# A Mamba and feed-forward kernel: two compares move to VectorE, the first block is reordered, the last block gets a path of its own

## The chip, the cores and the metric

The kernel runs on one core of a Trainium2 chip. The metric is the device time of one execution in microseconds (us). A core has five engines with a queue each, and each queue is worked off in order: TensorE (PE; its weight loads are listed as PEld), VectorE (DVE), ScalarE (ACT), GpSimd (POOL) and SyncE (SP), which here issues almost all DMAs. An instruction that waits holds up everything behind it in its queue.

## The reference

The input x has 2 sequences of 4096 tokens with 256 numbers each, all fp32. Two layers follow one another, both with a layer norm ahead and behind, and a residual:

```python
x = x + layernorm(mamba(layernorm(x)))
x = x + layernorm(ffn(layernorm(x)))

# mamba, 512 channels, 16 states
xp, z = split(x @ W_in.T);  xp = silu(xp)
B, C, dt_in, lam_in = split(xp @ W_x.T)         # 16, 16, 1, 1 columns
B, C = rmsnorm(B + B_bias), rmsnorm(C + C_bias)
dt = softplus(dt_in * W_dt + b_dt);  lam = sigmoid(lam_in)
B, C = rotate(B, C by the running sum of mean(dt))
dA = exp(-exp(A_log) * dt)
h[t] = dA[t] * h[t-1] + u[t]      # u from lam, dt, dA, B, xp of t and t-1
y = sum over states of h * C;  y = (y + xp * D) * silu(z)
return y @ W_out.T

# ffn, hidden 1024; ternary(w): the sign of w where |w| is over half its mean, times the mean
h = gelu(ln(x) @ ternary(w1).T + b1)
return ln(h) @ ternary(w2).T + b2
```

## The kernel before

The 8192 tokens are worked off in 16 blocks of 512. In a block the recurrence is 64 **units**: 4 groups of 128 channels (j), 4 rounds of states (q), 4 parts (c). Every unit is one scan on VectorE (`unit_scan`, L997 and L1000) over 512 tokens in 128 lanes. Its decay dA comes from ScalarE into one of four PSUM banks (`decay`, pool `ps_da`), its input from GpSimd as a product of b and v (`inputs`, L984, two units at a time). Afterwards the states are multiplied by c, partly on VectorE (L1014), partly on GpSimd (L1010), and TensorE sums them over the states into the bank of y (`sum_states`, L1026). There are three buffers of scan inputs; the sum frees one. After the 16 units of a channel group `gate` (L1036) multiplies y by silu(z).

The order of the work is written out by hand. Each unit has three **places**; the tables `AT`, `AT_FIRST`, `LAG` and `W_AT` give every step its place, and the program issues the steps in that order, so that each engine's queue follows it. While block k is scanned, `plan_ahead` prepares block k+1 (layer norm, projection, b, c, dt, v) and `plan_behind` finishes block k-1 (output projection, norm, the feed-forward layer). `AT_FIRST` is the table for block 0; its negative places lie before the first scan. After the last block 100 more units of places are run through with no scans, so that `plan_behind` finishes it.

What the steps of the change touch:

- Weights of the feed-forward layer (`ternary`, during block 0, for w1 and then w2): `above` and `below` (L410, L413) compare 128x2048 weights with plus and minus half of their mean on GpSimd, `signs` (L418) subtracts the two on GpSimd in two halves, `factors` (L423) scales two columns there; then TensorE sums the offsets (`offsets`, L445 and L466), VectorE adds them to the bias (L455, L476), ScalarE applies the gains (L456, L479).
- First block: `project` (L612) and `keep` (L626) make eight projections; the first four are copied to `xp`, on which `silu_x` then runs as one activation of 128x2048 (L225). `bc_project` (L643) multiplies `xp` by W_x, 128 tokens after another, each over all four channel groups. From its columns come dt (`dt_project`, `dt_row`, `dt_spread`, `softplus`), its transposes with sums (`dt_turn` L733, `dt_keep` L741), b and c (`bc_take` to `bc_store`), and v (`weigh` L865, `weigh_x` L880). dt, v, b and c are stored to DRAM (L708, L881, L812) and loaded back into lanes (`load_ch` L950 for dt and v, `load_bc` L939 for b and c), four DMAs per load. Several functions are loaded into ScalarE as tables (ACT_TABLE_LOAD); `special` (L225, with L221 for exp and ln) is the helper for these.
- Last block: `out_project` (L1044), `out_square` (L1056), `out_power`, `residual` (L1067), the norm (`Norm`: L557, L558, L562, L567, L572), its transposes (L586, L593), `ffn_1` and `ffn_keep` (L1072, L1083), `gelu` (L225), `ffn_2` (L1094, L1103, L1111), `ffn_sums` (L1120, L1124), `ffn_out` (L1132), `ffn_square` (L1141), `ffn_scale` (L1152), `finish` (L1156) and the store of half a block (L1157). The result of `ffn_2` for 128 tokens lies in the only bank of the pool `ps_ff`; the projections use the two banks of `ps_mm`.

Of the kernel before, what the change touches and what calls it, by code (L numbers as in the profile page):

```python
# [125 lines left out]
    "a_stats": (-60, -60),  # L126
    "a_power": (-60,),
    "a_offset": (-60,),
    "a_apply": (-60, -60),
    "a_turn": (-60, -60),  # L130
    "a_evict": (-60, -60),
    "project": (-59, -58, -57, -56, 16, 2, 2, 0),
    "keep": (-58, -57, -56, -55, 18, 3, 5, 0),
    "silu_x": (-54,),
    "bc_project": (-53, -53),
    "bc_take": (-52,),
    "dt_project": (-51,),
    "bc_square": (-50,),
    "bc_power": (-48,),
    "dt_row": (-49,),  # L140
    "dt_spread": (-48,),
    "softplus": (-47,),
    "bc_scale": (-46,),
    "dt_sum": (-45,),
    "dt_turn": (-46, -46, -46, -46),
    "dt_keep": (-46, -46, -46, -46),
    "angles": (-44,),
    "diag_lam": (-43,),
    "diag_rem": (-42,),
    "silu_z": (57,),  # L150
    "sines": (-40,),
    "rotate_a": (-37,),
    "rotate_b": (-36,),
    "bc_turn": (-34,),
    "bc_store": (-33,),
    "dot_sum": (-26,),
    "dot_shift": (0,),
    "dot_take": (0,),
    "weigh": (-41, 4, 10, 15),
    "weigh_x": (-35, 5, 11, 18),  # L160
# [3 lines left out]
    "load_dt": (-34,),  # L164
    "load_v": (-32,),
    "load_b": (-31, -20, 15, 3),
    "load_c": (-30, -20, 9, 4),
# [4 lines left out]
def mamba_ffn_kernel(  # L172
# [207 lines left out]
    def ternary(src, wide, nk, width, cols):  # L380
# [28 lines left out]
        def above():  # L409
            nc.gpsimd.tensor_scalar(q, w, t["scale"], 0.5, ALU.mult, ALU.is_gt)  # L410

        def below():
            nc.gpsimd.tensor_scalar(w, w, t["scale"], -0.5, ALU.mult, ALU.is_lt)  # L413
# [180 lines left out]

    class Block:
# [24 lines left out]
    def keep(s, e):  # L620
        if e == 0:
            s.xp = p1.tile([P, NJ, T], F32, tag="xp", name=f"xp_{s.k}")
            s.zs = {}
        if e >= NJ:
            s.zs[e - NJ] = p1.tile([P, T], F32, tag="zs", name=f"zs_{s.k}_{e - NJ}", bufs=8)
        nc.scalar.copy(s.xp[:, e, :] if e < NJ else s.zs[e - NJ], s.pz.pop(e))  # L626

    def silu_x(s):
        special(s.xp, s.xp, AF.Silu)
        s.xlast = small.tile([P, NJ], F32, tag="xlast", name=f"xlast_{s.k}")  # L630
        nc.scalar.copy(s.xlast, s.xp[:, :, T - 1])
# [5 lines left out]
    def bc_project(s, cs):  # L637

        if cs[0] == 0:
            s.pbc = ps_ff.tile([P, NC4, 2 * NS + 2], F32, tag="ff", name=f"pbc_{s.k}")  # L640
        for c in cs:
            for j in range(NJ):
                nc.tensor.matmul(  # L643
                    s.pbc[:, c, :],
                    lhsT=s.xp[:, j, c * P : (c + 1) * P],
                    rhs=wx[:, j, :],
                    start=(j == 0),
                    stop=(j == NJ - 1),
                )

# [384 lines left out]
    def gate(s, j):  # L1035
        nc.vector.tensor_mul(s.zs[j], s.ys.pop(j), s.zs[j])  # L1036

# [25 lines left out]
    def residual(s, h):  # L1063
        po, rs = s.p2.pop(h), s.ff["rso", h]
        for i in range(2):
            xc = s.x[:, 2 * h + i, :]
            nc.vector.scalar_tensor_tensor(xc, po[:, i, :], rs[:, i : i + 1], xc, ALU.mult, ALU.add)  # L1067
# [21 lines left out]
    def ffn_2(s, c):  # L1089

        po = ps_ff.tile([P, DM + 1 + P], F32, tag="ff", name=f"pf_{s.k}_{c}")
# [66 lines left out]

    NU = NJ * NQ * NG
# [17 lines left out]
    def plan_ahead(s, prev):  # L1177
# [24 lines left out]
        add("bc_project", bc_project, s, (0, 1), i=0)  # L1202
        add("bc_project", bc_project, s, (2, 3), i=1)
# [43 lines left out]
    def plan_behind(s):  # L1247
# [4 lines left out]
        def begin():  # L1252
            s.x = x_load(s.k, "xpost")

# [94 lines left out]
    first.run(-60)  # L1349
# [17 lines left out]
    decay_rates()  # L1367
# [7 lines left out]
    for base in range(NB * NU + BEHIND):  # L1375
# [3 lines left out]
        if m == 0:  # L1379
# [4 lines left out]
            if 0 < k <= NB:  # L1384
# [16 lines left out]
        at_place(3 * base + 2)  # L1401
        if m == X_AT and k + 2 < NB:
            xnext = x_load(k + 2, "h1")

# [47 lines left out]
```

## Time and profile before

| | |
|---|---|
| median of 3 runs | 2060.76 us (2060.21 to 2062.78) |
| the profiled execution's own time | 2060.96 us |
| its span, first to last instruction | 2059.2 us |
| first scan of block 0 | 64.26 us |
| first scan of block 1, of block 2 | 228.91, 345.65 us |
| POOL's wide compares, together | 28.7 us in four instructions |
| last gate (L1036) begins | 1987.59 us |
| last `finish` (L1156) ends | 2056.10 us |

The profile comes from one execution. Its page gives the busy time of each engine, the span in 40 slices (each digit is a busy share in tenths, `PEclk` the granted clock of TensorE in tenths), the chain of work that ended last, and the costliest groups of instructions. Other views are the timeline (start, duration, engine, line, operation, output and inputs; in brackets the idle time of the engine before it and who ended it), the waits (who waited for whom), and sums over chosen windows. Durations of neighbours in a queue overlap by up to 0.1 us, so steps from start to start are what adds up.

### The profile page before, as it was taken

Reading aid. Unit: us, or ns where it says so; the run is one execution under the profiler, and the core shown is the slowest. Engines: PE = TensorE matmul, PEld = TensorE weight load, DVE = VectorE, ACT = ScalarE, POOL = GpSimd, SP = SyncE. Lnnn points to the kernel's source line nnn. Section 1 sums busy time; section 2 is a strip of 40 time slices with the busy share of each in tenths; the row PEclk is TensorE's granted clock in tenths of the full one; section 3 lists DMA queues with packets and bytes.
Section 4 is the critical chain, followed back from the end, with each engine's and each line's share of the span. In section 5 each row is a group of like instructions: output and inputs, shape, how many; then the busy total and the mean of one; then the engine's idle time right before and its main releaser. Section 6 shows DMA issues by size and latency. Waiting matters only on the chain.

```text
span 2059.2 us, 28149 instructions
## 1 busy us (share of the span) xinstructions
PE 1742.7 (85%) x8638; PEld 1036.3 (50%) x8638; DVE 1761.0 (86%) x2766; ACT 1627.1 (79%) x3344; POOL 1815.7 (88%) x1178
## 2 busy tenths in 40 slices
PE   5755788898998989898888989899898889887776
PEld 3423436464563646455453646455464646545255
DVE  1654999999898999999999999999898999989950
ACT  5664797888979798887979788887978888896743
POOL 3599999899999999899999999999999999999950
PEclk7765899999999999999999999999999999999889
DMA  3632446345463645445444644446354545545200
GB/s 79 173 92 72 114 103 165 101 100 130 114 153 88 161 102 123 108 115 149 112 126 102 165 103 111 116 119 159 96 142 103 131 108 116 140 113 151 46 21 11
DMA packets 155689, 233.39 MB, mean 113 GB/s; under 512 B 30129, under 2 KB 55793, under 8 KB 155537
## 3 DMA queue, kind: packets, MB, share of 16 engines
q1 hardware_dynamic: 153408, 230.80, 45.0%
q0 software_dynamic: 544, 0.71, 0.2%
q8 instruction: 68, 1.11, 0.2%
q14 instruction: 85, 0.69, 0.1%
q10 hardware_dynamic: 1584, 0.07, 0.1%
HBM read 188.51 MB, written 42.99 MB: 112 GB/s over the span
## 4 chain that ended last, share of the span: by engine, by line
ACT 38%; DVE 17%; POOL 12%; DMA 11%; PE 11%; issue 8%; SPq 3%; DVEq 0%; ACTq 0%; POOLq 0%
ACT da L225 12%; POOL g L984 6%; DVE g L1000 6%; DMA vr<-v_d 6%; ACT L225 5%; DVE da L997 4%; ACT L221 3%; DMA xpre<-in_L_attn_x_dram 3%; ACT h L1083 3%; POOL g L1010 2%; ACT dt L225 2%; PE pdtT L733 2%; PE y L1026 2%; ACT h L225 2%; DVE g L1014 2%
## 5 line engine op out<-in xcount | busy, mean ns | idle before, releaser
L984 POOL TENSOR_TENSOR g<-b,vr 128x1024 f32<-128x1024 f32 x512 | 1017.4, 1999 | 36.1 <-DMA c<-bc_d 12.9
L1000 DVE TENSOR_TENSOR_SCAN g<-da,ini,g 128x512 f32<-128x512 f32 x560 | 709.9, 1272 | 46.4 <-ACT da L225 30.6
L225 ACT ACTIVATE da<-dtr,aneg 128x512 f32<-128x512 f32 x1024 | 683.7, 683 | 82.6 <-DVE g L1000 44.6
L1010 POOL TENSOR_TENSOR g<-c,g 128x1024 f32<-128x1024 f32 (+1 forms) x256 | 626.8, 2451 | 64.0 <-ACT hl L1004 55.0
L997 DVE TENSOR_TENSOR_SCAN da<-da,ini,g 128x512 f32<-128x512 f32 x336 | 422.0, 1274 | 33.2 <-POOL g L984 17.8
L1026 PE MATMUL y<-g,fold 128*32 128x512 f32 x2048 | 338.7, 662 | 42.3 <-POOL g L1010 32.2
L1094 PE MATMUL pf<-w2q,h 128*128 128x257 f32 x1024 | 313.4, 388 | 25.1 <-DVE o L1132 22.0
L1072 PE MATMUL ph<-oT_h,w1q 128*128 128x512 f32 x512 | 255.7, 635 | 24.8 <-ACT oT_h L593 13.3
L612 PE MATMUL pz<-oT_a,wi 128*128 128x512 f32 x512 | 251.0, 627 | 10.4 <-ACT zs L626 4.9
L1014 DVE TENSOR_TENSOR g<-da,c 128x512 f32<-128x512 f32 x384 | 257.3, 670 | 0.0
L1103 PEld LDWEIGHTS pf<-h 128*128 128x128 f32 x1024 | 194.6, 190 | 27.2
L1103 PE MATMUL pf<-h 128*128 128x128 f32 x1024 | 196.7, 274 | 0.0
L1094 PEld LDWEIGHTS pf<-w2q,h 128*128 128x128 f32 x1024 | 155.1, 191 | 61.1 <-DVE o L1132 42.1
L1072 PEld LDWEIGHTS ph<-oT_h,w1q 128*128 128x128 f32 x512 | 94.8, 200 | 164.5 <-issue 82.3
L612 PEld LDWEIGHTS pz<-oT_a,wi 128*128 128x128 f32 x512 | 92.9, 195 | 158.6 <-issue 87.3
L1026 PEld LDWEIGHTS y<-g,fold 128*32 128x32 f32 x2048 | 49.1, 112 | 155.8 <-POOL g L1010 66.0
L1044 PE MATMUL po<-wo,zs 128*128 128x256 f32 x512 | 120.9, 390 | 0.0
L1044 PEld LDWEIGHTS po<-wo,zs 128*128 128x128 f32 x512 | 96.2, 193 | 39.9 <-issue 27.6
L1000 DVE TENSOR_TENSOR_SCAN g<-da,g 128x512 f32<-128x512 f32 x80 | 96.5, 1211 | 19.7 <-ACT da L225 11.7
L865 PE MATMUL ps<-mix,dtT 128*128 128x129 f32 (+1 forms) x512 | 81.3, 306 | 34.2 <-DVE remdot L833 27.0
L865 PE MATMUL pw<-ddot,dtT 128*128 128x128 f32 (+1 forms) x512 | 83.8, 313 | 27.8 <-DVE dx L928 22.2
L225 ACT ACT_TABLE_LOAD x80 | 102.6, 1283 | 1.4
(209 smaller groups left out, 2390.4 us busy)
## 6 DMA issues: line engine op xcount, KB each, us to landing
dtr<-dt_d SPq DMA_DIRECT2D x256, 256.0 KB, 5.0
vr<-v_d SPq DMA_DIRECT2D x256, 256.0 KB, 7.1
dt_d<-dt SPq DMA_DIRECT2D x64, 256.0 KB, 2.1
v_d<-v SPq DMA_DIRECT2D x64, 256.0 KB, 4.8
b<-bc_d SPq DMA_DIRECT2D x256, 64.0 KB, 2.1
c<-bc_d SPq DMA_DIRECT2D x256, 64.0 KB, 2.7
xpre<-in_L_attn_x_dram SPq DMA_DIRECT2D x16, 512.0 KB, 4.3
xpost<-in_L_attn_x_dram SPq DMA_DIRECT2D x16, 512.0 KB, 3.8
```

Source lines behind the costliest of these rows:

```text
L225: nc.scalar.activation(dst, src, f, **kw)
L612: nc.tensor.matmul(s.pz[e], lhsT=wi[:, kk, e * P : (e + 1) * P], rhs=s.na.oT[:, kk, :], start=(kk == 0), stop=(kk == 1),)
L984: nc.gpsimd.tensor_mul(s.g[j, q][:, hs, :], s.bcq[0, q][:, None, :].to_broadcast([P, 2, T]), s.ch[j, "vr"][:, hs, :],)
L997: nc.vector.tensor_tensor_scan(da, da, g, ini, ALU.mult, ALU.add)
L1000: nc.vector.tensor_tensor_scan(g, da, g, ini, ALU.mult, ALU.add)
L1010: nc.gpsimd.tensor_mul(g, s.bcq[1, q][:, None, :].to_broadcast([P, NG - n, T]), g)
L1014: nc.vector.tensor_mul(s.g[j, q][:, c, :], da, s.bcq[1, q])
L1026: nc.tensor.matmul(s.ys[j][c * G : (c + 1) * G, :], lhsT=fold, rhs=g[:, c, :], start=False, stop=(q == NQ - 1), skip_group_check=True,)
L1044: nc.tensor.matmul(s.p2[h][:, i, :], lhsT=s.zs[j][:, c * P : (c + 1) * P], rhs=wo[:, j, :], start=(j == 0), stop=(j == NJ - 1),)
L1072: nc.tensor.matmul(s.ph[f], lhsT=w1q[:, kk, f * P : (f + 1) * P], rhs=s.nh.oT[:, kk, :], start=(kk == 0), stop=(kk == 1),)
L1094: nc.tensor.matmul(po[:, 0 : DM + 1], lhsT=gT, rhs=w2q[:, f, :], start=(f == 0), stop=(f == NH - 1), skip_group_check=True,)
L1103: nc.tensor.matmul(po[:, DM + 1 :], lhsT=gT, rhs=gT, start=False, stop=False, skip_group_check=True,)
```

## The change

The two compares of each weight run on VectorE instead of GpSimd. In block 0 `keep` applies silu while it takes the projection from PSUM, `bc_project_first` runs group by group between the projections, the norm of b and c follows softplus, dt's load stands directly behind its stores, and b is loaded ahead of v. The last block has no `plan_behind`: `tail` does its work, by halves of 256 tokens up to the gelu, with `ph` and `pf` in the four banks of `ps_da`, and stores 128 tokens at a time; three quarters of its output projection are issued at the gate of the third channel group. `residual` also writes row sums, in every block.

```diff
 AT_FIRST = {
...
-    "project": (-59, -58, -57, -56, 16, 2, 2, 0),
-    "keep": (-58, -57, -56, -55, 18, 3, 5, 0),
-    "silu_x": (-54,),
-    "bc_project": (-53, -53),
-    "bc_take": (-52,),
-    "dt_project": (-51,),
-    "bc_square": (-50,),
-    "bc_power": (-48,),
-    "dt_row": (-49,),
-    "dt_spread": (-48,),
-    "softplus": (-47,),
-    "bc_scale": (-46,),
-    "dt_turn": (-46, -46, -46, -46),
-    "dt_keep": (-46, -46, -46, -46),
+    "project": (-78, -77, -75, -72, 16, 2, 2, 0),
+    "keep": (-76, -74, -71, -69, 18, 3, 5, 0),
+    "silu_x": (-58,),
+    "bc_take": (-67,),
+    "dt_project": (-66,),
+    "bc_square": (-61,),
+    "bc_power": (-60,),
+    "dt_row": (-65,),
+    "dt_spread": (-64,),
+    "softplus": (-63,),
+    "bc_scale": (-59,),
+    "dt_turn": (-55, -55, -55, -55),
+    "dt_keep": (-55, -55, -55, -55),
...
-    "load_dt": (-34,),
-    "load_v": (-32,),
-    "load_b": (-31, -20, 15, 3),
-    "load_c": (-30, -20, 9, 4),
+    "load_dt": (-62,),
+    "load_v": (-42,),
+    "load_b": (-43, -20, 15, 3),
+    "load_c": (-41, -20, 9, 4),
+    "bc_project_first": (-73, -70, -69, -68),
+    "decay_rates": (-57,),
 }
...
         def above():
-            nc.gpsimd.tensor_scalar(q, w, t["scale"], 0.5, ALU.mult, ALU.is_gt)
+            nc.vector.tensor_scalar(q, w, t["scale"], 0.5, ALU.mult, ALU.is_gt)
         def below():
-            nc.gpsimd.tensor_scalar(w, w, t["scale"], -0.5, ALU.mult, ALU.is_lt)
+            nc.vector.tensor_scalar(w, w, t["scale"], -0.5, ALU.mult, ALU.is_lt)
...
+        if s.k == 0 and e < NJ:
+            special(s.xp[:, e, :], s.pz.pop(e), AF.Silu)
+            return
...
+    def bc_project_first(s, j):
+        if j == 0:
+            s.pbc = ps_ff.tile([P, NC4, 2 * NS + 2], F32, tag="ff", name=f"pbc_{s.k}")
+        for c in range(NC4):
+            nc.tensor.matmul(
+                s.pbc[:, c, :],
+                lhsT=s.xp[:, j, c * P : (c + 1) * P],
+                rhs=wx[:, j, :],
+                start=(j == 0 and c == 0),
+                stop=(j == NJ - 1),
+                skip_group_check=True,
+            )
...
     def gate(s, j):
         nc.vector.tensor_mul(s.zs[j], s.ys.pop(j), s.zs[j])
+        if s.k == NB - 1 and j >= NJ - 2:
+            tail_out(s, range(NJ - 1) if j == NJ - 2 else (j,))
...
     def residual(s, h):
...
-            nc.vector.scalar_tensor_tensor(xc, po[:, i, :], rs[:, i : i + 1], xc, ALU.mult, ALU.add)
+            nc.vector.scalar_tensor_tensor(
+                xc, po[:, i, :], rs[:, i : i + 1], xc, ALU.mult, ALU.add, accum_out=s.sums[:, c : c + 1]
+            )
...
+    def tail_out(s, js):
+        for h in range(2):
+            if 0 in js:
+                s.p2[h] = mm_tile([P, 2, DM], f"po_{s.k}_{h}")
+            for j in js:
+                for i in range(2):
+                    c = 2 * h + i
+                    nc.tensor.matmul(
+                        s.p2[h][:, i, :],
+                        lhsT=s.zs[j][:, c * P : (c + 1) * P],
+                        rhs=wo[:, j, :],
+                        start=(j == 0 and i == 0),
+                        stop=(j == NJ - 1),
+                        skip_group_check=True,
+                    )
+    def tail(s):
...
+        for h in range(2):
+            out_square(s, h)
+            out_power(s, h)
+        for h in range(2):
+            cl = slice(2 * h, 2 * h + 2)
+            residual(s, h)
+            n.stats((2 * h, 2 * h + 1))
+            power(n.rs[:, cl], n.var[:, cl], n.scale, n.eps)
+            nc.vector.tensor_mul(n.nm[:, cl], n.nm[:, cl], n.rs[:, cl])
+            n.apply((2 * h, 2 * h + 1))
...
+        for h in range(2):
+            for f2 in range(NH // 2):
+                ph = ps_da.tile([P, 2, T // 2], F32, tag="da", name=f"ph_{k}_{h}_{f2}")
...
+                for i in range(2):
+                    f = 2 * f2 + i
+                    special(s.h1[:, f, half[h]], ph[:, i, :], AF.Gelu, bias=b1c[:, f : f + 1])
+        for c in range(NC4):
+            ffn_2(s, c, ps_da.tile([P, DM + 1 + P], F32, tag="da", name=f"pf_{k}_{c}"))
...
+        for c in range(NC4):
+            ffn_sums(s, c)
+            ffn_out(s, c)
+            junk = p1.tile([P, DM], F32, tag="junk", name=f"junk_{k}_{c}")
+            nc.scalar.activation(junk, s.o2[:, c, :], AF.Square, accum_out=so[:, c : c + 1])
+            power(rg[:, c : c + 1], so[:, c : c + 1], 1.0 / DM, LN_EPS)
+            xc = s.x[:, c, :]
+            nc.vector.scalar_tensor_tensor(
+                xc, s.o2[:, c, :], rg[:, c : c + 1], xc, ALU.mult, ALU.add
+            )
+            nc.sync.dma_start(tokens(out, k)[:, c, :], xc)
...
-            if 0 < k <= NB:
+            if 0 < k < NB:
                 plans.append(plan_behind(prev))
...
+        if base == NB * NU - 10:
+            tail_load(cur)
...
+    tail(blocks[NB - 1])
```

In `tail`, `n` is a `Norm` whose statistics come from ScalarE: the mean from the row sums that `residual` wrote, the variance from a Square with that mean as its bias and an accumulator. The transposes of each half are taken from PSUM by one copy on VectorE. `tail_load` reads the last block's x into a free buffer of dt ten units before the last scan.

## The prediction

> **What bounds the kernel now.** The page first. Times are microseconds from the span's start.
>
> ```profile
> PE 1742.7 (85%) x8638; PEld 1036.3 (50%) x8638; DVE 1761.0 (86%) x2766; ACT 1627.1 (79%) x3344; POOL 1815.7 (88%) x1178
> ...
> DVE  1654999999898999999999999999898999989950
> POOL 3599999899999999899999999999999999999950
> PEclk7765899999999999999999999999999999999889
> ```
>
> GpSimd (POOL) and VectorE (DVE) are busy together all through the middle; only the first four slices and the last two are thin. So the windows view comes next, by stage (busy time of PE, weight loads, DVE, ACT, POOL, then the granted clock):
>
> ```profile
> 101.00:228.90 127.90, 70.47 (x282) 38.96 (x282) 76.45 (x116) 71.44 (x144) 121.71 (x69) 0.65 0.34 84
> 376.30:463.90 87.60, 76.85 (x397) 45.35 (x397) 81.28 (x131) 75.77 (x161) 82.63 (x56) 0.96 0.46 114
> 1988.30:2059.20 70.90, 49.91 (x207) 35.35 (x206) 6.90 (x24) 25.71 (x61) 2.73 (x3) 0.91 0.05 16
> ```
>
> Counting scans in the timeline, the first row holds the last 48 scans of block 0, the second the same 48 of block 2: 127.9 against 87.6. The third row is the last block after its last gate: 70.9 in which no engine but PE does much. The change works at the start (nothing scans before 64.26), in block 0, and at the end. The steady blocks hardly change.
>
> In block 0 POOL's timeline and VectorE's waits say who is to blame:
>
> ```profile
> 118.07 7.18 POOL L410 TENSOR_SCALAR wide<-wide,scale 128x2048 f32<-128x2048 f32 x1
> ...
> 134.05 7.16 POOL L413 TENSOR_SCALAR wide<-wide,scale 128x2048 f32<-128x2048 f32 x1
> 141.30 2.34 POOL L418 TENSOR_TENSOR wide<-wide 128x1024 f32<-128x1024 f32 x1
> ```
> ```profile
> 145.63 2.35 DVE L997 TENSOR_TENSOR_SCAN da<-da,g 128x512 f32<-128x512 f32 x2 [9.19 <-POOL g L984]
> ...
> 200.93 0.42 DVE L476 TENSOR_TENSOR b2bc<-pb,b2bc 128x256 f32<-128x256 f32 x1 [15.82 <-PE pb L466]
> ...
> 215.00 2.29 DVE L502 SCALAR_TENSOR_TENSOR wide<-pm,wide 128x2048 f32<-128x2048 f32 x1 [0.28 <-ACT m L499]
> ```
>
> Four compares of 7.17 sit in GpSimd's queue ahead of the products that the scans need; each time VectorE runs dry (5.65, 9.19, 6.24, 15.82).
>
> At the start, the timeline:
>
> ```profile
> 21.59 1.28 ACT L225 ACT_TABLE_LOAD   x1
> 22.89 1.91 ACT L225 ACTIVATE xp<-xp 128x2048 f32<-128x2048 f32 x1
> ...
> 24.85 6.82 PE L643 MATMUL pbc<-wx,xp 128*128 128x34 f32 x32 [3.90 <-ACT xp L225]
> ```
>
> PE stands 3.9 for the silu; the windows by 2 us show its clock at 1.00 to 24 and 0.50 from 26 on, and the 32 matmuls then step by 0.213. (The median step of L643 over all blocks is 0.112.)
>
> **Part 1, compares on VectorE.** Removed from POOL: 4 x 7.17 = 28.7. Added to DVE: four tensor_scalars of 128x2048. The trace has none on DVE. Bounds: nothing, since DVE idles here (it can hide in a wait), and above, the only DVE row of that size, L502, 2.29. I take 2.29: same size, same engine. The gain by following the queues:
> - L410 of the first weight: POOL's next product moves from 126.12 to about 121, but DVE used that wait to work off scans till 125.4 and now has 2.3 more. It reaches the scan of 131.01 at 128: gain 3.
> - L413: DVE reaches it at 131.0 and ends it at 133.3. The subtraction L418 on POOL waits for it (a new wait: queued behind it are the next products), 2.34, then a product of 1.96: the scan of 145.63 starts at 137.6. Gain so far 8.
> - Second weight: mean, scale and inverse at 173.1 come at 165.1. The inverse ends at 165.6; compare, scan, compare (2.3 + 1.1 + 2.3) end at 171.3; POOL's L418 twice and the two factors (4.63 + 0.6) end at 176.5. L466 on PE takes 5.67 (it began at half clock, after 22.5 of waiting), so b2bc comes at 182.2 instead of 200.93. DVE has three scans left before it (to 175.6): still a wait of 6.6 in place of 15.8, and ACT's L479 waits beside it. That is late next.
> So **18.7**. With compares at nothing, 18.7 + 4 x 2.3 = 27.9, the fast end. Slow end: all four compares lie on the path and each costs another 1.3, two thirds of a product of 2.0 that it meets in flight: 18.7 - 5.2 = 13.5.
>
> [...]
>
> **Part 2, first block.** Silu takes each projection from PSUM (0.58 copy becomes about 0.67, a quarter of 1.91 plus the fixed part that 0.58 shows), its table load moves ahead of the first projection, where ACT waits from 13.6 to 15.84. The 32 small matmuls go between the projections (8 after each), so PE no longer stands, and at clock 1.00 they step by 0.11. Chain re-timed with the rows' durations, before to after:
> - projections done 20.97 to 22.0 (one group of 0.9 goes ahead of the fourth); pbc done 31.68 to 24.5.
> - dtrow 33.49 to 25.9; softplus's table load follows it directly; dt starts 36.45 to 27.9, ends at 30.6.
> - now the squares and powers of b and c stand between dt and dtT on ACT: table load 1.28, exp, a round through POOL and DVE, two powers, xlast, decay rates, 3.4 in all. dtT done 43.0 to 37.1: of 8.6 gained, 2.7 is given back.
> - v stored 48.45 to 42.6; b and c stored 52.01 to 44.7. SP's queue: dt's loads are issued from 31 on, long before; b waits for its store (2.1) and is issued at 46.9, 4 x 0.44; v's loads 48.6, behind b although v landed at 44.7: 2 are lost there. v then lands at about 55 (dt's 1 MB no longer shares the engines; before, issue of 52.49 landed at 61.35).
> - first product 62.22 to 55.3, first scan 64.26 to 57.3. The next scans hang on ACT's and PE's chain from bct (zs, ddot, dx, v of the second group), which moves from 50.03 to 44.1.
> So **6**. Bounds: 3, if PE's clock falls anyway (pbc at 27.8 and the chain 3.3 later); 9, if v lands with b.
>
> [...]
>
> **Part 3, last block.** Now: the last gate ends at 1988.28, the end is at 2059.2. Four ffn_2 groups of 5.6 run one after another with 1.7 to 2.9 between, as one bank holds them:
>
> ```profile
> 2027.52 0.29 DVE L1120 SCALAR_TENSOR_TENSOR junk<-pf,ident 128x128 f32<-128x128 f32 x1 [27.51 <-PE pf L1111]
> ...
> 2036.22 0.29 DVE L1120 SCALAR_TENSOR_TENSOR junk<-pf,ident 128x128 f32<-128x128 f32 x1 [5.83 <-PE pf L1111]
> ```
>
> After:
> - tail_out for three quarters at gate 2 (1966.98): 24 matmuls of 0.216 = 5.2, queued on PE behind ffn_2 (ends 1971.02) and ahead of the sum of 1970.94. That sum frees the buffer for POOL's last inputs: 1973.25 to 1977.2. Scans and products end about 2.2 later; but PE then doesn't idle 4.1 before the last sum, which took 1.93 at clock 0.50 and takes 0.95. Last gate ends at 1989.4, **1.1 later**.
> - remaining 8 matmuls 1.8 (first half at 1990.4); squares, powers, residual, statistics, apply by halves on ACT in one queue: first half turned at 1998.0, second at 2001.4 (now 2005.06).
> - ffn_1 by halves: 64 matmuls of 128x256, the first 4.2 us at half clock (as now, steps of 0.85 up to 2007.84): 1998.0 to 2013.9. Gelu from PSUM with bias, 128x256 (L520's 0.49, 0.40 in sequence), keeps pace. Now: 2022.6 to its end at 2024.3.
> - ffn_2 four times without gaps, 4 x 5.56: 2036.2 (now 2051.1).
> - last tile: 0.3 + 0.67 + 0.5 + 0.6 + 0.5 + 0.46 to 2039.6; store to end 3.1 as now (2056.1 to 2059.2): 2042.7.
> So **16.5**. Bounds: 12 (tail_out delays the gate by 4, its whole wait for the buffer, and ACT's queue by 1.5 more), 19 (no delay, half clock absent).
>
> **Elsewhere.** residual gets an accumulator in 15 blocks, 60 reads. L1120's read shows 0.083, but the next scan starts with it (1980.96 both): bounds 0 and 60 x 0.083 = 5, where DVE is the late one; I take **1**.
>
> **Sum.** 6 + 18.7 + 16.5 - 1 = 40.2 off the profiled execution's 2060.96 (span 2059.2 and 1.8 around it): 2020.8; its time is 0.2 above the median of the runs, so 2020.6.
>
> **Rivals.**
> - [...] 0.16.
> - The end gains half: tail_out holds up the last sums and the half-wide matmuls pay for it at half clock, 8 instead of 16.5: 2029.1. 0.12.
> - The start gains nothing, since v's load now waits for b's store as well: 2026.6. 0.05.
> - All better than I count: under 2010.4. 0.05.
> - The other side: the accumulator in residual, on the engine that bounds 15 blocks. It turns the sign if each of 60 costs over (40.2 + 1)/60 = 0.69, as much as a product of 128x512 (L1014's 0.67); L1120's read shows 0.083. At 0.8 each: 2067.6. 0.02; within 0.2%, 0.01.
> - My forecast, about 2010 to 2026: 0.59.
>
> 0.2% (4.1) is about what a measurement tells from no change. Faster 0.97, same 0.01, slower 0.02. The range of 8 in 10: fast end with compares at nothing and the accumulator free, 6 + 27.9 + 16.5 = 50.4, so 2010.4; slow end with every term at its slow bound and 4 for the accumulator, 3 + 13.5 + 12 - 4 = 24.5, so 2036.3. It holds the first three rivals; all fast ends at once are left out.
>
> **What would show it.** Right: pbc done near 24.5 with steps of 0.11; first scan near 57; no POOL wide row but L418; DVE's wait before b2bc about 6; scan 49 of block 0 near 176.6 instead of 201.27; last gate within 3 of now; ffn_2 in one run of 22 on PE. Wrong: steps of 0.21 in pbc, a compare far over 2.3, POOL rows that stretch beside a compare, blocks 1 to 14 longer than 117 each, PE waiting in ffn_2.

## The result, and the profile after

The changed kernel takes **2028.12 us** (median of 4 runs, 2024.18 to 2030.12), the kernel before took 2061.77 beside it: a ratio of 0.9833, 95% interval 0.9814 to 0.9852, or 33.6 us less (30.5 to 38.3). The forecast was 2020.6, a gain of 40.2, so the sign and most of the size came, and 6.6 us of the expected gain did not. The profiled execution took 2027.52, its span is 2025.8.

The busy line of the page after, and its slices of TensorE's granted clock:

```profile
PE 1739.3 (86%) x8670; PEld 1039.7 (51%) x8670; DVE 1769.0 (87%) x2834; ACT 1624.4 (80%) x3358; POOL 1786.3 (88%) x1171
...
PEclk7867999999999999999999999999999999999798
```

GpSimd lost 29 us of work and VectorE gained only 8. The last row is the one to watch: TensorE's granted clock is still low in the first four slices and again near the end.

The windows view by the same three stages as before (the last 48 scans of block 0, the same 48 of block 2, the stretch from the last gate's start, where the row of before began at the gate's end; columns as before: PE, weight loads, DVE, ACT, POOL, then the granted clock):

```profile
94.60:199.93 105.33, 70.53 (x279) 38.23 (x280) 82.15 (x121) 71.26 (x144) 94.15 (x65) 0.68 0.41 103
350.00:435.10 85.10, 74.30 (x375) 42.84 (x375) 78.80 (x129) 73.36 (x149) 80.53 (x55) 0.96 0.45 111
1967.90:2025.80 57.90, 44.33 (x216) 37.93 (x216) 9.08 (x29) 24.65 (x76) 0.00 (x0) 0.85 0.04 14
```

These scans of block 0 went from 127.9 to 105.3 with GpSimd at 94 instead of 122; the end, counted from the last gate's start in both, from 71.6 to 57.9. TensorE's clock is 0.85 there, where 0.91 was before. (The second row starts 2.6 us into the 48 scans; from first to last they take 87.7, as before.)

Counting scans in the timeline gives the time by stage:

| stage | before | after | difference | forecast |
|---|---|---|---|---|
| to the first scan | 64.26 | 59.60 | -4.7 | -7.0 |
| block 0 | 164.66 | 140.33 | -24.3 | -17.7 |
| blocks 1 to 14 | 1644.40 | 1648.74 | +4.3 | +1 |
| block 15 to the end | 185.85 | 177.12 | -8.7 | -16.5 |

So the compares gave more than I said, the start and the end less, and the steady blocks took something back. One profile of each kernel doesn't settle such differences: runs of one kernel spread by some 6 us here. The experiments do.

**The theory** for the shortfall: TensorE's clock. At the start and at the end TensorE works in short pieces with waits between, its clock falls to half (0.50 in the windows view from 28 to 50 us and from 1968 to 1972), and every piece that lies on the path doubles. **The rivals**: at the end, `tail_out` delays the last gate, or the two halves don't overlap; at the start, the loads of v wait behind b; in blocks 1 to 14, the accumulator in `residual` costs.

### The profile page after: what moved, and what is told of

Read it like the earlier page. It is cut to its first block, busy times and chain, and to the rows that moved or that the text cites. A ratio compares the mean times of both kernels' runs of the same rounds, so it can differ in the third digit from the quotient of the medians.

```text
span 2025.8 us, 28291 instructions
## 1 busy us (share of the span) xinstructions
PE 1739.3 (86%) x8670; PEld 1039.7 (51%) x8670; DVE 1769.0 (87%) x2834; ACT 1624.4 (80%) x3358; POOL 1786.3 (88%) x1171
## 4 chain that ended last, share of the span: by engine, by line
ACT 38%; DVE 18%; PE 13%; POOL 11%; DMA 10%; issue 7%; SPq 2%; DVEq 0%; ACTq 0%; POOLq 0%
ACT da L227 12%; DVE g L1046 6%; POOL g L1030 6%; DMA vr<-v_d 5%; ACT L227 5%; DVE da L1043 4%; ACT L223 3%; ACT h L1134 3%; DMA xpre<-in_L_attn_x_dram 2%; POOL g L1056 2%; ACT dt L227 2%; PE y L1072 2%; PE pdtT L779 2%; DVE g L1060 2%; PE pz L639 2%
## 5 line engine op out<-in xcount | busy, mean ns | idle before, releaser
L1146 PE MATMUL pf<-w2q,h 128*128 128x257 f32 x1024 | 312.9, 387 | 18.2 <-DVE o L1184 14.9
L1123 PE MATMUL ph<-oT_h,w1q 128*128 128x512 f32 x480 | 242.1, 639 | 24.1 <-ACT oT_h L595 13.1
L1123 PEld LDWEIGHTS ph<-oT_h,w1q 128*128 128x128 f32 x480 | 89.1, 201 | 156.2 <-issue 75.8
L1092 PE MATMUL po<-wo,zs 128*128 128x256 f32 x480 | 111.6, 386 | 0.0
L1092 PEld LDWEIGHTS po<-wo,zs 128*128 128x128 f32 x480 | 88.7, 190 | 36.8 <-issue 26.0
L779 PE MATMUL pdtT<-ident,dt 128*128 128x128 f32 x256 | 54.6, 357 | 57.7 <-ACT dtT L787 32.6
```

Source lines behind the costliest of these rows:

```text
L1092: nc.tensor.matmul(s.p2[h][:, i, :], lhsT=s.zs[j][:, c * P : (c + 1) * P], rhs=wo[:, j, :], start=(j == 0), stop=(j == NJ - 1),)
L1123: nc.tensor.matmul(s.ph[f], lhsT=w1q[:, kk, f * P : (f + 1) * P], rhs=s.nh.oT[:, kk, :], start=(kk == 0), stop=(kk == 1),)
L1146: nc.tensor.matmul(po[:, 0 : DM + 1], lhsT=gT, rhs=w2q[:, f, :], start=(f == 0), stop=(f == NH - 1), skip_group_check=True,)
```

## The experiments

### One part at a time

Four kernels are the kernel before with one part each. First the compares alone:

```diff
-            nc.gpsimd.tensor_scalar(q, w, t["scale"], 0.5, ALU.mult, ALU.is_gt)
+            nc.vector.tensor_scalar(q, w, t["scale"], 0.5, ALU.mult, ALU.is_gt)
-            nc.gpsimd.tensor_scalar(w, w, t["scale"], -0.5, ALU.mult, ALU.is_lt)
+            nc.vector.tensor_scalar(w, w, t["scale"], -0.5, ALU.mult, ALU.is_lt)
```

> The kernel before, with the four compares on VectorE and nothing else. My theory, from the two traces: the compares alone give most of what the whole change gave between the first scan and block 1, so first scan unchanged at 64.3, first scan of block 1 at about 205.5 instead of 228.9, time about 2038 (-23). Rival: the gain in block 0 came half from the earlier start (loads and PE clock better placed), then block 1 starts at 212 to 216 and the time is about 2046 to 2049. A compare that meets a running POOL product takes 1.1 more than one that meets an idle POOL (1.27).

Measured 2042.62 against 2063.72: ratio 0.9898 (0.9884 to 0.9912), **21.1 us less** (18.2 to 23.9). Block 0 takes 140.37, about what it takes in the whole change (140.33), and the wait before b2bc is 6.73. Block 1 starts at 204.48, so the rival falls.

The second has the first block's new order alone (the table `AT_FIRST`, `bc_project_first`, silu from PSUM):

```diff
-    "load_v": (-32,),
-    "load_b": (-31, -20, 15, 3),
+    "load_v": (-42,),
+    "load_b": (-43, -20, 15, 3),
...
+            for j in range(NJ):
+                add("bc_project_first", bc_project_first, s, j, i=j)
```

> The kernel before, with the first block's new order alone (silu from PSUM, small matmuls between the projections, dt and b ahead of v). My theory: first scan at 59.6, third scan 5.2 earlier, and since the compares on POOL then bound block 0 and their places are tied to the units, the 5 are carried through to the end: time about 2056 (-5). Rival: block 0 is bound by GpSimd's sum of work from the first product on; the same 5 then, but if the weights' DMAs and ACT steps bound it, they come no earlier and the gain is lost in block 0: 2060 to 2061.

Measured 2061.65 (11 runs): ratio 0.9988 (0.9980 to 0.9997), **2.1 less** (0.6 to 4.1). Its profile has the first scan at 59.27, 5.0 earlier, and block 1 starts at 222.15 where three other kernels with the old start and the old compares have 226.4 to 228.9. So the gain is there at the end of block 0 in that profile, which was taken at 2057.64, 4.0 below the median; the median shows less than half. That profile can't say what the other runs lost, and this stays open.

The third has the last block's path alone (`tail`, `tail_out`, `tail_load`, and the accumulator in block 15 only):

```diff
+        if s.k == NB - 1 and j >= NJ - 2:
+            tail_out(s, range(NJ - 1) if j == NJ - 2 else (j,))
...
+    tail(blocks[NB - 1])
```

> The kernel before, with the last block's own path alone (accumulator in residual only in the last block). My theory: from the last gate to the end 57.9 instead of 71.6, the last gate itself 2.9 later because of the output projection queued ahead of the sum that frees POOL's buffer: time about 2050 (-11). Rival: the 8.8 that the whole change showed from block 15 on is all that the tail can give, 2052, and the rest was chance.

Measured 2050.59: ratio 0.9938 (0.9924 to 0.9951), **13.1 less** (10.1 to 15.7). That is more than the rival's 8.8. From block 15 to the end it takes 177.2; the four kernels with the old end take 185.9 to 188.4. That is 8.7 to 11.2 less; where the rest of the 13.1 comes from is not shown.

The fourth has only the accumulator in `residual`, whose sums nobody reads:

```diff
-            nc.vector.scalar_tensor_tensor(xc, po[:, i, :], rs[:, i : i + 1], xc, ALU.mult, ALU.add)
+            nc.vector.scalar_tensor_tensor(
+                xc, po[:, i, :], rs[:, i : i + 1], xc, ALU.mult, ALU.add, accum_out=s.sums[:, c : c + 1]
+            )
```

> The kernel before, with row sums written by residual in 15 blocks and nothing else that uses them. Theory A: blocks 1 to 14 were 4.3 longer after the change because TensorE's clock was at half in one stretch of ffn_1 in more of the blocks, which is chance from run to run; the accumulator costs under 1: 2061 to 2062. Theory B: the accumulator costs 0.3 per block, or tips the schedule: 2065 to 2066.

Measured 2065.16 (11 runs): ratio 1.0006 (0.9997 to 1.0015), 1.4 more, not told from nothing, and theory B's 4 to 5 lie outside the interval. At the accumulator's own place, units 16 to 20, the fourteen blocks take 144.6 to 144.7 in all ten profiles that have it and 143.9 in the four that don't: 0.7 in sum. The whole of blocks 1 to 14 settles less: 1648.75 here, but in the profiles of the four kernels whose steady blocks have no accumulator 1644.4, 1645.7, 1645.9 and (the tail alone) 1648.85. The same blocks differ by 4.4 from profile to profile, so the 4.3 can't be put down to the accumulator.

The four parts add to -34.9, the whole gives -33.6: within the intervals, they don't act on one another.

### What the end lost

Five rows of the changed kernel's PE timeline, from the first part of the output projection on (start, duration, ..., what it waited for):

```profile
1948.31 5.35 PE L1225 MATMUL po<-wo,zs 128*128 128x256 f32 x24
1953.58 1.06 PE L1072 MATMUL y<-g,fold 128*32 128x512 f32 x8
...
1965.86 1.93 PE L1072 MATMUL y<-g,fold 128*32 128x512 f32 x6 [2.85 <-POOL g L1056]
1968.64 3.78 PE L1225 MATMUL po<-wo,zs 128*128 128x256 f32 x8 [0.85 <-DVE zs L1082]
...
1981.09 16.49 PE L1267 MATMUL ph<-oT_h,w1q 128*128 128x256 f32 x64
```

The 5.35 stand ahead of the sum that frees GpSimd's buffer. GpSimd waits for it, as its timeline says:

```profile
1954.82 3.96 POOL L1030 TENSOR_TENSOR g<-b,vr 128x1024 f32<-128x1024 f32 x2 [4.08 <-PE y L1072]
```

The last sum still takes 1.93 for six passes, where eight took 1.06 at 1953.58; the remaining projection takes 3.78 instead of 1.8. Both ran at a clock of 0.50. And VectorE's timeline shows why the first half gains nothing on the second:

```profile
1979.27 0.16 DVE L1250 TENSOR_TENSOR nm_h<-nm_h,rs_h 128x2 f32<-128x2 f32 x1 [2.33 <-ACT rs_h L227]
1979.35 0.69 DVE L1259 COPY oT_h<-pt_h 128x512 f32<-128x512 f32 x1
```

The copy of the first half's transposes (done at 1978.05) is queued behind the second half's mean times factor, and ffn_1 behind the second half's transposes: both halves of the norm are issued before any transpose. The two causes, and the delay of the gate, were undone one at a time in the changed kernel. The intervals of these kernels' times overlap with its own. But block 15 to the end takes 176.97 to 177.20 in the four profiles with this end and unaltered steady blocks, so that a microsecond there can be read from one profile.

**The halves in order**: first half's norm, transposes and ffn_1 are issued ahead of the second half's norm.

```diff
-        for h in range(2):
-            residual(s, h)
...
+        norm_half(0)
+        turn_half(0)
+        ffn_half(0)
+        norm_half(1)
+        turn_half(1)
+        gelu_half(0)
+        ffn_half(1)
+        gelu_half(1)
```

> The changed kernel, with the last block's queues reordered so that the halves really overlap: first half's transposes, its copy and its ffn_1 are issued ahead of the second half's. My theory: in the changed kernel ffn_1 of the first half stands behind the second half's transposes on TensorE and its copy behind the second half's norm on VectorE, 3.9 of the 7.7 by which the last block's gain missed the forecast; so ffn_1 starts 2.3 earlier and the end comes about 2 earlier (1 to 3): 2026. Rival: TensorE's ffn_1 starts at half clock in any case and the second half's transposes then wait behind the first half's ffn_1: no gain, 0 to +1.

Measured 2027.65 (2024.10 to 2028.23), ratio 0.9825 (0.9811 to 0.9838); the profile has 175.97 from block 15 to the end, 1.15 less than 177.12. ffn_1 starts 2.2 earlier from the start of the block, but its first half now runs nearly throughout at half clock:

```profile
1980.76 9.10 PE L1270 MATMUL ph<-oT_h,w1q 128*128 128x256 f32 x32 [0.78 <-DVE oT_h L1262]
1989.69 0.60 PE L1259 MATMUL pt_h<-ident,o_h 128*128 128x128 f32 x4
1991.17 7.14 PE L1270 MATMUL ph<-oT_h,w1q 128*128 128x256 f32 x32 [0.88 <-DVE oT_h L1262]
```

**PE kept busy**: matmuls of the identity into a bank of the decays that is free by then, which nobody reads; 3 ahead of the last sum and 5 behind the last part of the output projection.

```diff
+                if s.k == NB - 1 and j == NJ - 1 and q == NQ - 1:
+                    keep_warm(s, 0, 3)
                 sum_states(s, j, q)
...
+    def keep_warm(s, i, n):
+        pw = ps_da.tile([P, T], F32, tag="da", name=f"warm_{i}")
+        for _ in range(n):
+            nc.tensor.matmul(pw, lhsT=ident, rhs=wi[:, 0, 0:T], start=True, stop=True)
```

> The changed kernel with eight matmuls of 128x512 whose result nobody reads: three on TensorE ahead of the last sum and five behind the last part of the output projection. My theory: they fill the idle stretches after which the granted clock falls to 0.50, so the last sum takes 1.0 instead of 1.9, the last part of the output projection 1.8 instead of 3.8 and ffn_1's first steps are 0.22 instead of 0.43: the end comes 4 to 5 earlier, 2023.5. Rival: the clock follows something else than idle time of TensorE, or the extra matmuls stand in the way: 0 to +2.

Measured 2025.09 (2021.84 to 2025.82), ratio 0.9814 (0.9801 to 0.9827); block 15 to the end 174.03, **3.1 less**:

```profile
1962.99 2.84 PE L1091 MATMUL warm<-wi,ident 128*128 128x512 f32 x6
1965.76 2.04 PE L1072 MATMUL y<-g,fold 128*32 128x512 f32 x8
1968.66 1.99 PE L1232 MATMUL po<-wo,zs 128*128 128x256 f32 x8 [0.85 <-DVE zs L1082]
1970.49 4.46 PE L1091 MATMUL warm<-wi,ident 128*128 128x512 f32 x10
```

The same eight passes of the output projection take 1.99 instead of 3.78. The clock is 1.00 from 1961 to 1970.6; the row of 2.04 holds two passes at 1965.76 and, behind a wait, the last six, which take 1.1 instead of 1.93. The last gate comes 0.85 earlier in its block. (One 128x512 matmul in fp32 is two passes of 0.43 in the records: 5 of them are the row "x10" of 4.46.)

**No early projection**: the whole output projection waits for the last gate.

```diff
-        if s.k == NB - 1 and j >= NJ - 2:
-            tail_out(s, range(NJ - 1) if j == NJ - 2 else (j,))
+        if s.k == NB - 1 and j == NJ - 1:
+            tail_out(s, range(NJ))
```

> The changed kernel with the whole output projection of the last block at its last gate, as in the kernel before, and the rest of the tail as changed. My theory: the 24 matmuls of 5.3 at the third gate hold up the sum that frees GpSimd's last buffer; without them the last gate comes 2.9 earlier, but they then stand behind it, the second half's squares wait 4.4 longer, and the end is 0 to 2 later: 2028 to 2030. Rival: moving them ahead gave most of the tail's gain: without it the end is 5 or more later.

Measured 2028.03, ratio 0.9833 (0.9819 to 0.9846), the same. The last gate comes 2.85 earlier in its block (116.38 instead of 119.23), the 32 passes then take 9.25 in one row, and the end is 0.9 later. So the early projection costs its 2.85 on the gate and is worth 3.7 behind it (61.6 from the gate to the end, where the changed kernel has 57.9).

**Both repairs together**:

> The changed kernel with both repairs of its end together: the order by halves and the eight idle-filling matmuls (3 ahead of the last sum, 5 behind the last part of the output projection). Theory: the shortfall of the end is half clock (3.1 in the profile with the filling) and the order of the halves (1.15 in the profile with the order); they lie one behind the other, so block 15 to the end is about 172.9 instead of 177.1, and the time about 2024. Rival: both gains are the same wait seen twice, so the end stays at 174.0 as with the filling alone, 2025.1.

Measured 2023.11 (2018.42 to 2024.84), ratio 0.9803 (0.9790 to 0.9817); block 15 to the end 171.59, 5.5 less than the changed kernel. With PE kept busy the order by halves is worth 2.4 instead of 1.15, as the first half of ffn_1 takes 7.17 instead of 9.10: they add, and a little more. The rival that both are the same wait falls.

### What the start lost

**v ahead of b**, in the changed kernel:

```diff
-    "load_v": (-42,),
+    "load_v": (-45,),
```

> The changed kernel, with v's load ahead of b and c's store and loads in SyncE's queue of the first block. My theory: v's store has landed by 46.5 but its load waits behind b until 50.75; with it first, v lands about 3.5 earlier, first scan at 56.1 instead of 59.6, and block 1 begins 2 to 3.5 earlier. Rival: the start isn't bound by v: the third scan waits for the chain through TensorE and ScalarE (zs, second v, dx) and block 0 takes up what comes earlier, so block 1 begins as now, within 1.

Measured 2028.37, ratio 0.9829 (0.9813 to 0.9845), the same; first scan at 59.16 instead of 59.60. The loads of v are issued at 46.15 instead of 50.75, but the store of b and c then lands 5.7 after its issue instead of 1.6, among the megabyte of v, and b is issued at 53.72 instead of 48.95. One of the two transfers is late in either order; the 2 us that I put down to v behind b were not lost. Block 1 begins at 199.25 instead of 199.93, as the rival said.

**PE kept busy at the start.** The changed kernel's PE timeline:

```profile
27.49 2.04 PE L709 MATMUL pb<-dtrow,ones 1*128 1x512 f32 x2 [0.76 <-ACT dtrow L704]
...
36.29 1.97 PE L779 MATMUL pdtT<-ident,dt 128*128 128x128 f32 x8 [2.55 <-ACT dtT L787]
...
39.54 1.42 PE L763 MATMUL pa<-msum,ones 128*128 128x3 f32 x6
```

The clock is 0.50 in every window of 2 us from 28 to 50. A first filling put 20 matmuls of 128x512 into the waits (twelve by this list, eight more at the transposes of dt):

```diff
+    "warm": (-67, -65, -63, -53, -46),
...
+            for i, n in enumerate((2, 2, 2, 2, 4)):
+                add("warm", first_warm, f"{i}", n, i=i)
```

> The changed kernel with 20 idle-filling 128x512 matmuls in the start of block 0, behind pbc, pdt and pb, between the transposes of dt, ahead of the cumulative sums and ahead of the rotation's transposes. Theory: my forecast of the start was short by 2.3 (first scan at 59.60 instead of 57.3) because PE ran at half clock from 27 to 51 us: pb 2.04 instead of 1.0, the second transposes of dt 1.97, the sums 1.4, ps 2.09; with the clock at 1.00 there the first scan is at about 57 and the time 2.5 lower, 2025.5. Rival: the transfers through DRAM set the first scan (b, then v, issued from 48.95 on, land no sooner than 57), so the first scan stays within 0.8 of 59.60 and the time at 2028.

Measured 2030.08, ratio 0.9841 (0.9827 to 0.9854), no gain: first scan at 62.48, **2.9 later**. The clock was 1.00, and pb took 1.12 instead of 2.04. But I had counted 0.43 for a 128x512 matmul, which takes twice that; the filling ran over the waits and stood ahead of the real work (pb began at 29.64 instead of 27.49). The run says that the filling was too large, and nothing on the rival.

### What the steady blocks lost

Here are two neighbouring blocks of the changed kernel, the last rows of PE ahead of the first ffn_1 (L1123) of blocks 5 and 6:

```profile
716.91 0.66 PE L588 MATMUL pt_h<-ident,o_h 128*128 128x128 f32 x4 [0.34 <-ACT zs L657]
718.01 1.98 PE L1123 MATMUL ph<-oT_h,w1q 128*128 128x512 f32 x4 [0.45 <-ACT oT_h L595]
...
834.69 0.66 PE L588 MATMUL pt_h<-ident,o_h 128*128 128x128 f32 x4 [0.34 <-ACT zs L657]
835.80 3.68 PE L1123 MATMUL ph<-oT_h,w1q 128*128 128x512 f32 x4 [0.45 <-ACT oT_h L595]
```

The same work with the same waits, and the same four passes take 1.98 in one block and 3.68 in the other. In every profile of this study the clock changes only at instants that lie whole multiples of 3.413 us apart (93 changes in the one before, 91 in the one after). The windows view on this grid, around the four rows (clock behind POOL's column):

```profile
712.99:716.40 3.41, 2.47 (x8) 1.10 (x8) 3.41 (x6) 3.41 (x9) 3.41 (x3) 1.00 0.00 0
716.40:719.81 3.41, 2.62 (x10) 1.09 (x8) 3.41 (x6) 3.41 (x8) 3.33 (x4) 1.00 0.02 5
...
832.46:835.87 3.41, 1.72 (x10) 0.91 (x9) 3.41 (x5) 3.41 (x9) 3.41 (x3) 1.00 0.00 0
835.87:839.28 3.41, 3.41 (x4) 1.05 (x4) 3.41 (x7) 2.31 (x4) 3.33 (x3) 0.50 0.00 0
```

In block 6 the thin stretch ahead of ffn_1 lies in one window, with PE busy 1.72 of 3.41, and the next window runs at half clock. In block 5 the boundary at 716.40 cuts the same stretch in two, with 2.47 and 2.62, and the clock stays at 1.00. The windows of all 14 profiles from 250 us on agree. Taking those at clock 1.00, half clock followed after all 194 in which PE was busy for less than 0.4 of the window, after 284 of the 693 between 0.4 and 0.6, and after 31 of the 5781 above 0.6. In 30 of these 31, PE was busy throughout, mostly with the narrow matmuls (128x34) of pbc.

The scans feel it: units 24 to 28 take 7.0 in most blocks and 8.2 in such a one. The waits ahead of the one in block 6 are single gaps of 0.90, 0.34 and 0.45 with short transposes between them. The change did not bring these stretches: in blocks 1 to 14 the profile before has 36 windows at half clock, the one after 37.

**Filling those gaps**: in blocks 0 to 14, matmuls of the identity into a bank that is free there, 2 ahead of the first transposes, 1 ahead of the second, 1 ahead of ffn_1.

```diff
+            if s.k < NB - 1:
+                add("h_turn", ffn_warm, s, h, (2, 1)[h], i=h)
             add("h_turn", lambda h=h: s.nh.turn(h), i=h)
...
     def ffn_1(s, f):
+        if f == 0 and s.k < NB - 1:
+            ffn_warm(s, 2, 1)
```

> The changed kernel with four idle-filling 128x512 matmuls in every block but the last, around the transposes ahead of ffn_1 (2 before the first four, 1 before the second four, 1 before ffn_1), into the bank that is free there. Theory: blocks 1 to 14 come out at 1648.7 or at 1645 because the tensor engine's clock halves for some 3.5 us at ffn_1 in some blocks only, by where its gaps of 0.91, 0.34 and 0.45 fall; with the gaps filled no block has its first ffn_1 row at 3.7, units 24 to 28 take 7.0 everywhere, and the 14 blocks take about 1641: 2020 to 2022. Rival 1: the blocks are set by VectorE and GpSimd, which never feel it: 1648 and 2028. Rival 2: the filling (4 x 0.43) delays the real matmuls by what it fills: each block up to 1.7 longer, up to 2050.

Measured 2028.52 (5 runs, 2019.33 to 2030.23), ratio 0.9831 (0.9818 to 0.9844): by the median, nothing. The profile, taken at 2019.33, has 1642.5 for blocks 1 to 14, but units 24 to 28 take 7.5 to 8.0 in all of them, 106.6 in sum where the changed kernel has 104.7: this filling was twice too large as well. What that profile won lies elsewhere (units 0 to 4 take 160.4 in sum instead of 164.5, units 32 to 36 102.3 instead of 107.9). Inconclusive.

**The filling cut to size**: the kernel with both repairs of the end, and both fillings with 128x256 instead of 128x512 (128x128 for the three between the first transposes of dt); at the start there are 17 of them instead of 20.

```diff
+    def first_warm(name, n, w=T // 2):
+        pw = ps_da.tile([P, T], F32, tag="da", name=f"warm_{name}")
+        for _ in range(n):
+            nc.tensor.matmul(pw[:, 0:w], lhsT=ident, rhs=wi[:, 0, 0:w], start=True, stop=True)
...
+            for i, n in enumerate((1, 1, 1, 2, 4)):
+                add("warm", first_warm, f"{i}", n, i=i)
```

> The kernel with both repairs of the end (2023.1), with the idle-filling of the start and of the steady blocks cut to the size of the gaps: a 128x512 matmul is two passes of 0.43, so the earlier fillings were 0.86 each, twice what I had meant; now 128x256 (0.43), and 128x128 between the transposes of dt. The profile tells the stages apart. Theory for the start (half clock costs it about 2.5): first scan at about 56.5; its rival (transfers set it): over 58.5. Theory for the steady blocks (half clock at ffn_1 in some of them): the interval of units 24 to 28 is 7.0 in all fourteen and they take about 1641 to 1643; its rival (filling costs what it saves): 1646 or more. End: 171.6 as before. If both theories hold, 2013 to 2016; if neither, 2023.

Measured **2013.62** (5 runs, 2011.18 to 2018.55), ratio 0.9771 (0.9756 to 0.9786), the fastest kernel of this study: 9.5 under the one with both repairs of the end, 14.5 under the changed kernel (6.6 and 12.8 by the ratios to the kernel before, which was measured beside each anew). Its profile, of the run at the median, by stage:

| stage | both repairs | with the fillings cut to size |
|---|---|---|
| to the first scan | 58.90 | 57.20 |
| block 0 | 142.31 | 140.85 |
| blocks 1 to 14 | 1648.97 | 1642.63 |
| block 15 to the end | 171.59 | 171.21 |

At ffn_1 of block 6, PE's timeline now reads:

```profile
833.31 0.60 PE L1154 MATMUL warm<-wi,ident 128*128 128x256 f32 x2
833.92 1.98 PE L1142 MATMUL ph<-oT_h,w1q 128*128 128x512 f32 x4
```

Units 24 to 28 take 7.0 in thirteen of the fourteen blocks and 7.2 in the other; over the fourteen this interval fell from 104.7 to 98.7, almost all of the 6.3. The clock agrees: five windows at half clock began in units 24 to 28 of these blocks, and none does now, though in all of blocks 1 to 14 there still are 35, where 36 were. The theory for the steady blocks holds. At the start, the rows that were at half clock:

```profile
35.92 1.23 PE L787 MATMUL pdtT<-ident,dt 128*128 128x128 f32 x8 [0.95 <-ACT dtT L797]
...
38.24 0.81 PE L769 MATMUL pa<-msum,ones 128*128 128x3 f32 x6
```

1.97 became 1.23 and 1.42 became 0.81. pb still took 2.07: the clock was 0.50 from 26 to 30. The first scan is at 57.20, where the theory said 56.5 and its rival over 58.5; the seven profiles with the new start and no filling there have 58.90 to 60.85. The start was limited by the half clock more than by the transfers.

## Why the prediction was right, and where it was short

**Part 1, compares: right, 18.7 forecast, 21.1 measured alone.** The step that was mis-sized is the one that took 2.29 for a compare, by L502 as the nearest row. VectorE's timeline of the changed kernel:

```profile
115.48 2.35 DVE L412 TENSOR_SCALAR wide<-wide,scale 128x2048 f32<-128x2048 f32 x1
...
123.54 1.27 DVE L415 TENSOR_SCALAR wide<-wide,scale 128x2048 f32<-128x2048 f32 x1
...
157.16 1.29 DVE L412 TENSOR_SCALAR wide<-wide,scale 128x2048 f32<-128x2048 f32 x1
...
159.50 1.26 DVE L415 TENSOR_SCALAR wide<-wide,scale 128x2048 f32<-128x2048 f32 x1
...
171.94 0.42 DVE L478 TENSOR_TENSOR b2bc<-pb,b2bc 128x256 f32<-128x256 f32 x1 [7.16 <-PE pb L468]
```

Three compares take 1.26 to 1.29. The row of 2.29 has two input tiles and the compare one. With 1.27 in place of 2.29 the same sum gives 22.8 (18.7 + 4 x 1.02), an estimate. The first compare takes 2.35, and GpSimd's timeline shows with whom it met:

```profile
113.84 2.91 POOL L1056 TENSOR_TENSOR g<-c,g 128x1536 f32<-128x1536 f32 x1 [1.74 <-ACT hl L1050]
116.71 2.98 POOL L1030 TENSOR_TENSOR g<-b,vr 128x1024 f32<-128x1024 f32 x1
```

The compare begins in the middle of the first product and lasts 1.1 longer than the others; that product ends at 116.75, 1.27 after the compare's start. The next product takes 2.98 where its like takes 2.0; it begins 1.12 ahead of the compare's end at 117.83. The kernel with the compares alone repeats it to the hundredth (2.35 and 2.98). Such a meeting came once in four compares; the other three, which met no product in flight, took 1.26 to 1.29. So the 1.3 that the slow end adds to each of the four is shown by no run: one of them took 1.1 longer. The wait before b2bc (forecast 6.6, 7.16 here) came as the queues said; scan 49 came 4.3 earlier than forecast (172.28 instead of 176.6). The rival of 0.16, by which the compares change their place and not their cost for a gain of 9, falls: 21.1.

**Part 2, first block: 6 forecast, 2.1 measured alone, 4.7 to 5.0 at the first scan.** pbc ran at clock 1.00 with steps of 0.11: that step was right, though pbc was done at 25.36 and not at 24.5, 0.9 late. The step that failed is what stands between dtrow and the store of b and c, at half clock. The forecast leaves pb 1.4 between dtrow's end (26.5) and dt (27.9), where the trace before has pb at 2.04; it took 2.04 again, and dt starts at 29.57, 1.7 late. The sums ran at clock 1.00 in the trace before (0.81 for six passes) and at 0.50 here (1.42). With these 0.6, b and c are stored at 47.29 instead of 44.7, 2.6 late, and the first scan comes 2.3 late. So some 1.4 of it is half clock; dtT, ps and the turn were at half clock in the trace before too, and the forecast had them so. The loss that I did count (v behind b) was none. That the median shows only 2.1 was not explained.

**Part 3, last block: 16.5 forecast, 13.1 measured alone, 8.7 in the profile after.** Right: ffn_2 in one run (22.07, forecast 22.2), store to end 3.1, ffn_1 by halves 16.5 (forecast 15.9). Failed, in two steps. "PE then doesn't idle 4.1 before the last sum, which took 1.93 at clock 0.50 and takes 0.95": it still idled 2.85 and took 1.93, and the remaining projection took 3.78 instead of 1.8; keeping PE busy gave back 3.1. "first half turned at 1998.0", 8.6 after the gate's end: ffn_1 began 12.5 after it, since the queues of VectorE and PE hold the second half's norm ahead of it; the order by halves gave back 1.15 alone and 2.4 with the clock up. The gate itself came 4.95 later in its block instead of 1.1; 2.85 of that are the early projection, as the kernel without it shows, and the other 2.1 are found in kernels with the old end as well (187.9 and 188.4 where the kernel before has 185.9); their cause stays open. A smaller slip: the terms of the last tile add up to 3.0 and not to the 3.4 written (2036.2 to 2039.6); 3.2 were measured.

**Elsewhere: +1 forecast.** The accumulator costs 1.4 at the median, between -0.6 and 3.1, and 0.7 at its own place. Of the +4.3 of blocks 1 to 14, 2.4 stand in units 24 to 36, where ffn_1's clock is felt, 0.8 in the accumulator's units and 0.8 in the first four; one kernel without the accumulator in these blocks has it too. That the rest is the clock is not shown.

The terms are off by -2.4, +3.9, +3.4 and +0.4, so the parts give 34.9 instead of 40.2; the whole gives 33.6. Half clock stood in the bounds of both terms that fell short, but not where it came: the start's 3 has it at pbc ("if PE's clock falls anyway"), which ran at 1.00; the end's sum has it in the first 4.2 us of ffn_1, and not in the last sum and the remaining projection.

There is some luck in the number: the compares' 2.4 more made up for part of what the other two lost. 2028.12 lies in the stated range, but past the span given to the forecast itself (about 2010 to 2026), between the values of two rivals (start gains nothing, 2026.6; end gains half, 2029.1). Neither came: the parts gave 2.1 and 13.1. Of the signs of being wrong, two came. A POOL row did stretch beside a compare, by 1.0, at no loss for the part. Blocks 1 to 14 take 117.8 each, over the 117 named, but that sign tells nothing, as they took 117.5 before. And of the signs of being right, the last gate is not within 3 of its place in the block, but 4.95 later.

## What to carry to other kernels

Where TensorE works in short pieces between waits, read its granted clock before pricing any of its rows, and price moved rows at the clock of the place that they move to. Matmuls that nobody reads, into a bank that is free, kept the clock up here (1.00 from 1961 to 1970.6 at the end, where it was 0.50 from 1965.7 on without them), and paid as long as they were no larger than the wait they filled: at the start and in the steady blocks, fillings of twice the size brought nothing in the time, and the first scan came 2.9 later. When work is split in halves to overlap, follow each engine's queue: what is issued for the second half ahead of the first half's next step undoes the split (1.15 to 2.4 us here).

## What the runs showed of the hardware

- The clock changed only on a grid of 3.413 us. A window of it at clock 1.00 with PE busy 1.72 of 3.41 was followed by one at half clock, while the same work cut by a boundary into 2.47 and 2.62 kept 1.00. Over the 14 profiles, of the windows at clock 1.00, all 194 with PE busy under 0.4 were followed by half clock, and 31 of the 5781 above 0.6, mostly those that PE spent on narrow 128x34 matmuls.
- Over fourteen blocks the intervals at ffn_1 sum to 104.7, and to 98.7 with the gaps filled.
- A one-input compare of 128x2048 fp32 takes 1.27 on VectorE and took 7.17 on GpSimd. Started inside a GpSimd product it took 2.35, and the product after it 2.98 instead of 2.0.
- The store of 64 KB for b and c landed in 1.6 after its issue, and in 5.7 with a megabyte of v issued just ahead of it.
- Four and more runs of one kernel spread by 3 to 8 us, and by 11 with the oversized filling in the steady blocks (2019.33 to 2030.23). That the place of the clock's windows is behind this spread would fit, but no run here tells it.
